# A gated recurrence in 128 steps: other queues for the first loads, biases loaded spread out, and plain units moved in the last steps

## The chip, the cores and the metric

The kernel runs on one core of a Trainium2 chip. The metric is the device time of one execution in microseconds, as the median of several runs; 0.2% of it is 2.7 us. The profile is that of one further execution with its own time. A core has five engines with queues of their own: TensorE (PE, with its weight loads as PEld), VectorE (DVE), ScalarE (ACT), GpSimd (POOL) and SyncE (SP). Loads and stores are issued here from SP's queue and from ScalarE's.

## The reference

A gated recurrent unit runs over 128 steps for 64 sequences with 512 inputs and 512 hidden values, and its outputs are added to the input:

```python
def step(h, inp):
    x_t, prop = inp
    comb = jnp.concatenate([x_t, h], axis=-1)
    z = jax.nn.sigmoid(comb @ Wz + bz)
    r = jax.nn.sigmoid(comb @ Wr + br)
    comb2 = jnp.concatenate([x_t, r * h], axis=-1)
    h_cand = jnp.tanh(comb2 @ Wh + bh)
    h_new = (1.0 - z) * h + z * h_cand
    h_next = jnp.where(prop, jnp.tanh(h_new @ Wp + bp), h_new)
    return (h_next, h_new)
```

`prop` holds at every fourth step except the last. The result is `x` plus all `h_new`. Everything is float32.

## The kernel before

**Layout.** The 64 sequences and two halves of the 512 hidden values together fill 128 partitions: partition `s * 64 + b` holds columns `256 s` to `256 s + 255` of sequence `b`. A product with one 128-row block of a weight matrix is two matmuls (`products`, L188), one for each half `s`, into the upper and the lower 64 partitions of PSUM; each is two float32 instructions of 256 columns. Such a pair of matmuls is called a unit. Four units make one gate of one step.

**The serial part.** A step multiplies h (turned into hT, k on partitions) by the lower rows of Wr, then Wz (`wh[0]`, `wh[1]`), takes sigmoids on ScalarE, forms `rh = r * h` on VectorE, turns it (`turn`, L213: eight transposes on TensorE and two copies), and multiplies it by the lower rows of Wh (`wh[2]`). Then come tanh, a multiplication by z and an addition of `keep = (1 - z) h`, each in two halves (c = 0, 1), and the turn of the new h, in two halves too. The slots for r and the candidate lie in one PSUM tile (`rc`), z's and the propagation's in another (`zp`). They are seeded ahead of the products with what x and the bias contribute to the step (`seed`, a ScalarE copy from `G[t]`), so that the products only accumulate.

**The parallel part.** What x contributes doesn't depend on h and fills TensorE's time while the other engines work through the chain. For steps 0 to 7 it is done plainly: `plain(t)` gives 12 units, four for each gate, from the upper rows of the weights (`wx`), and VectorE then adds the bias into `G[t]`. From step 8 to 123 four steps are taken together with sums of weights and sums of inputs that save products (`batch`, with GpSimd doing most additions). The last four steps are plain again (`plain_last`). The units stand in a list, and `fill(n)` issues the next n of them at the place where it is called. The program order written out by hand is thus the order of every engine; `manual_schedule` leaves it alone. `read_out()` emits the additions that take finished units out of PSUM.

**Places.** In steps up to 118 `PLACES` says how many units go to which place of a step. In the last nine steps, 119 to 127, `TAIL` does: its first triple holds the units ahead of the first half turn of h, between the two half turns, and behind the second. The second pair serves the propagation.

**The start.** Ten idle matmuls on zeros run while the first loads arrive. The four biases arrive as four rows in one partition (`bias_row`, which borrows the space of the weight sums `tt`). `spread` multiplies them by a row of ones, so that they stand in all 64 rows of each half in PSUM, directly in the slots of step 0, and copies them to `bias`. Then `turn_x` turns x of steps 0 and 1. Step 0's units accumulate straight into the biased slots, one by one alternating with the plain units of step 1. h's first state is turned after r's units. The upper rows of each weight matrix are loaded in two halves, the first on SP's queue and the second on ScalarE's. ScalarE's queue starts with the biases and carries the first state after its half of Wr. The lower rows all go on SP's queue, in the order r, x of steps 2 and 3, z, candidate.

**Order on the other engines around the change.** At step 3 VectorE does `sum_inner(5)` and `sum_inner_1(5)` (L320 to L325) after its copy for the turn of h and ahead of the read-out of a finished batch (L515 to L517). At step 127 ScalarE seeds the candidate's slot (L395, called at L666) ahead of the sigmoid of r (L675).

Of the kernel before, what the change touches and what calls it, by code (L numbers as in the profile page):

```python
# [9 lines left out]
F32 = mybir.dt.float32  # L10
BF16 = mybir.dt.bfloat16
# [6 lines left out]
def kernel(  # L18
# [29 lines left out]
    nc = tc.nc  # L48
# [20 lines left out]
    ps_c = ctx.enter_context(tc.tile_pool(name="ps_c", bufs=1, space=PSUM))  # L69
    ctx.enter_context(tc.manual_schedule())  # L70

    ident = const.tile([P, P], F32, name="ident")
    make_identity(nc, ident)
    ones = const.tile([1, B], F32, name="ones")
# [9 lines left out]
    tw = {n: const.tile([P, S, S, 3, P], F32, name=f"tw_{n}") for n in (2, 3, 4)}  # L84
    tt = const.tile([P, 7, 3, S, 3, P // 2], F32, name="tt")
    gates_in = (Wr, Wz, Wh)

    bias_row = tt.rearrange("p a b c d e -> p (a b c d e)")[0:1, : 4 * H].rearrange(
        "p (i n) -> p i n", i=4
    )  # L90

    def load_x(tile_, t0, n, j=0):
        for s in range(S):
            nc.sync.dma_start(
                out=tile_[s * B : (s + 1) * B, j : j + n, :], in_=x[:, t0 : t0 + n, ts(s, N)]
            )

    def load_w(wt, w, k0, k1, eng):
        eng.dma_start(
            out=wt[:, k0:k1, :],  # L100
            in_=w[k0 * P : k1 * P, :].rearrange("(k p) n -> p k n", p=P),
        )
# [3 lines left out]
    def new_xr(g):  # L106
        xr[g] = xrp.tile([P, Q4, N], F32, tag="xr", name=f"xr_{g}")

    for i, b in enumerate((br, bh, bz, bp)):
        nc.scalar.dma_start(out=bias_row[:, i, :], in_=b.rearrange("(o n) -> o n", o=1))  # L110
    h_init = two.tile([P, N], F32, tag="h", name="h_init")
    new_xr(0)
    load_x(xr[0], 0, 2)
    for i in range(3):
        for k in (0, 2):
            load_w(wx[:, :, i, :], gates_in[i], k, k + 2, nc.sync if k == 0 else nc.scalar)
        if i == 0:
            for s in range(S):
                nc.scalar.dma_start(out=h_init[s * B : (s + 1) * B, :], in_=h0[:, ts(s, N)])
    for i in range(3):  # L120
        for k in (0, 2):
            load_w(wh[i], gates_in[i][D:, :], k, k + 2, nc.sync)
        if i == 0:
            load_x(xr[0], 2, 2, 2)

    dummy = const.tile([1, 1], F32, name="dummy")
    nc.scalar.activation(dummy, ones[:, 0:1], AF.Sigmoid)
# [23 lines left out]
    act_ps = [ps[:, N : N + P] for ps in turn_ps]  # L151


    bias = const.tile([P, C, 4, P], F32, name="bias")

    def cut(ps):
        return ps.rearrange("p (c n) -> p c n", c=C)

    def spread(a, ps):
        for s in range(S):  # L160
            nc.tensor.matmul(  # L161
                ps[s * B : (s + 1) * B, :, :],
                lhsT=ones,
                rhs=bias_row[:, 2 * a : 2 * a + 2, ts(s, N)],
                start=True,
                stop=True,
            )
        for i in ((R, H_), (Z, 3))[a]:
            nc.vector.tensor_copy(bias[:, :, i, :], cut((slots[i] if i < 3 else slot_p)))  # L169

    bias0 = bias[:, 0, 0:3, :]
    bias_d = const.tile([P, 3, P], F32, name="bias_d")


    zeros = one.tile([P, 2 * N], BF16, tag="cq", name="zeros")
    nc.gpsimd.memset(zeros, 0.0)

    def idle(n):
        for _ in range(n):
            nc.tensor.matmul(  # L180
                scratch[0][:B, :], lhsT=zeros[:, :B], rhs=zeros, start=True, stop=True
            )


# [208 lines left out]
    def seed(i, t):  # L393
        if t < T:
            nc.scalar.copy(cut(slots[i]), G[t][:, :, i, :])  # L395
# [5 lines left out]
    def fill(n):  # L401
        for _ in range(min(n, len(queue))):
            unit, end = queue.pop(0)
            unit()
            if end is not None:
                pending.append(end)
# [5 lines left out]
    def plain(t):  # L412

        first, second = scratch[:2] if t % 2 == 0 else scratch[2:]
        regions = (first[:, :N], first[:, N:], second[:, :N])
        g, i = divmod(t, Q4)

        def end():
            new_cp(t // 2)
            nc.vector.tensor_add(  # L420
                G[t][:, :, 0:2, :],
                first.rearrange("p (g c n) -> p c g n", g=2, c=C),
                bias[:, :, 0:2, :],
            )
# [119 lines left out]
        nc.gpsimd.tensor_add(dst, a, b)  # L544

    def with_bias(g, i, v):
        m = M[g, i].rearrange("p b g u -> p b (g u)")
        nc.gpsimd.tensor_add(
            m, m, v.rearrange("p g u -> p (g u)").unsqueeze(1).to_broadcast([P, 2, 3 * P])
        )  # L550

    def c_block(g, a, nb):
# [28 lines left out]
    def outer_c21(g):  # L581
# [7 lines left out]


    TAIL = (
        ((4, 1, 0), (2, 1)), ((4, 1, 0), ()), ((4, 1, 0), ()), ((4, 1, 0), ()),
        ((4, 1, 0), (2, 1)), ((4, 1, 0), ()), ((5, 1, 2), ()), ((3, 1, 0), ()), ((0, 0, 0), ()),
    )


    idle(10)
    spread(0, rc)
    turn_x(0, nc.vector)
    turn_x(1, nc.vector)  # L600
    spread(1, zp)
    nc.gpsimd.tensor_sub(bias_d, bias[:, 1, 0:3, :], bias0)
    idle(2)
    h = h_init
    hT = new_T("hT", "hT_init")
    first = [
        [lambda e=e, k=k: product(slots[e], xT[0][:, 0], wx[:, :, e, :], k) for k in ORDER]
        for e in range(3)
    ]
    second = plain(1)  # L610
    for e in range(3):

        queue.extend(second[4 * e : 4 * e + 4])
        for n in range(4):
            first[e][n]()
            fill(1)
        if e == 0:
            for c in range(C):
                turn(h, hT, c, "hT_init", nc.vector)
    read_out()  # L620
# [3 lines left out]
    for t in range(T):  # L624
# [37 lines left out]
        if t < 6:  # L662
            turn_x((2, 5, 8, 11, 13, 15)[t])
        read_out()
        if t == T - 1:
            seed(H_, t)  # L666
        if u == 0 and pair >= 1 and odd - 2 < LAST:
            outer_u2(odd - 2)
        if t == 3:
# [4 lines left out]
        for c in range(C):  # L674
            nc.scalar.activation(act_ps[c], slots[R][:, ts(c, P)], AF.Sigmoid)  # L675
            nc.vector.tensor_mul(rh[:, ts(c, P)], act_ps[c], h[:, ts(c, P)])  # L676
        seed(R, t + 1)
        join(0)


# [12 lines left out]
        nc.scalar.activation(slots[Z], slots[Z], AF.Sigmoid, scale=-1.0)  # L693
        nc.vector.tensor_mul(keep, slots[Z], h)
        join(1)
        seed(Z, t + 1)
        if prop:
            nc.scalar.copy(cut(slot_p), bias[:, :, 3, :])
# [37 lines left out]
        fill(places[2] if thin else places[1] - 6)  # L736
        if t == 2:
            sum_outer_1()
        if t == 3:
            sum_inner(5, nc.vector)  # L740
            sum_inner_1(5, nc.vector)
        if prop:
            for k in ORDER:
                product(slot_p, hT, wp, k)
# [128 lines left out]
```

## Time and profile before

| what | us |
| --- | --- |
| median of three runs | 1343.7 |
| lowest and highest run | 1342.44, 1344.1 |
| the profiled execution | 1342.88 |
| its span, first to last instruction | 1341.0 |
| TensorE busy | 1329.3 |
| GpSimd busy | 908.7 |
| VectorE busy | 702.2 |
| ScalarE busy | 626.6 |

The span is what the profile's times count in; the execution's own time is 1.9 us longer. The mean granted TensorE clock is 0.998. A row of the timeline gives the start, the duration, the engine with the line, the operation, the tile written and the tiles read, the shape and how many instructions were merged; in brackets stands how long the engine sat idle ahead of it and what ended that. Lines are those of the kernel before. L188 is the matmul of `products`, L213 a transpose of `turn`, L204 the copy that follows it, L180 an idle matmul, L161 a bias matmul, L395 a seed. Matmuls overlap, so one row's duration is more than its share of TensorE's time: 16 instructions of 256 columns with 379 ns each take 1.73 us, hence 0.43 us for a unit.

### The profile page before, as it was taken

Reading aid. Unit: us, or ns where it says so; the run is one execution under the profiler, and the core shown is the slowest. Engines: PE = TensorE matmul, PEld = TensorE weight load, DVE = VectorE, ACT = ScalarE, POOL = GpSimd, SP = SyncE. Lnnn points to the kernel's source line nnn. Section 1 sums busy time; section 2 is a strip of 40 time slices with the busy share of each in tenths; the row PEclk is TensorE's granted clock in tenths of the full one; section 3 lists DMA queues with packets and bytes.
Section 4 is the critical chain, followed back from the end, with each engine's and each line's share of the span. In section 5 each row is a group of like instructions: output and inputs, shape, how many; then the busy total and the mean of one; then the engine's idle time right before and its main releaser. Section 6 shows DMA issues by size and latency. Waiting matters only on the chain.

```text
span 1341.0 us, 37605 instructions
## 1 busy us (share of the span) xinstructions
PE 1329.3 (99%) x15344; PEld 1113.4 (83%) x15344; DVE 702.2 (52%) x1868; ACT 626.6 (47%) x1848; POOL 908.7 (68%) x1111
## 2 busy tenths in 40 slices
PE   9999999999999999999999999999999999999998
PEld 6678888888888888888888888888888888888765
DVE  3355555555555555555555555555555555555444
ACT  1244545454554545455445454545445444554433
POOL 3448776777767777776787767787677687767400
PEclk9999999999999999999999999999999999999999
DMA  9011223122221222213212231222212222131300
GB/s 286 18 33 33 64 47 80 35 49 49 64 65 33 65 42 56 64 33 71 57 34 65 53 76 33 49 48 65 64 33 65 48 49 64 33 80 34 103 18 17
DMA packets 114868, 76.22 MB, mean 57 GB/s; under 512 B 61700, under 2 KB 109956, under 8 KB 114696
## 3 DMA queue, kind: packets, MB, share of 16 engines
q1 hardware_dynamic: 113632, 72.04, 23.2%
q8 instruction: 121, 1.98, 0.6%
q10 hardware_dynamic: 1064, 1.78, 0.4%
q14 instruction: 51, 0.42, 0.1%
HBM read 42.34 MB, written 16.78 MB: 44 GB/s over the span
## 4 chain that ended last, share of the span: by engine, by line
PE 99%; DVE 1%; issue 0%; ACT 0%; POOL 0%; DVEq 0%; POOLq 0%; ACTq 0%
PE rc L188 34%; PE zp L188 20%; PE scratch_q L188 11%; PE scratch_x L188 11%; PE scratch_r L188 10%; PE scratch_a L188 6%; PE turn L213 5%; PE scratch_q L180 0%; PE rc L161 0%; ACT xT L204 0%; PE zp L161 0%; DVE rh L676 0%; DVE turn L720 0%; DVE bias L169 0%; DVE h L725 0%
## 5 line engine op out<-in xcount | busy, mean ns | idle before, releaser
L188 PE MATMUL rc<-wh,rhT 128*64 128x256 f32 x2048 | 245.9, 379 | 0.0
L188 PE MATMUL zp<-wh,hT 128*64 128x256 f32 x1536 | 204.5, 379 | 0.0
L188 PEld LDWEIGHTS rc<-wh,rhT 128*64 128x64 f32 x2048 | 167.4, 137 | 41.1
L544 POOL TENSOR_TENSOR cp<-mb,mb 128x768 f32<-128x768 f32 x72 | 130.8, 1816 | 102.4 <-ACT rc L395 54.8
L188 PE MATMUL rc<-wh,hT 128*64 128x256 f32 x1536 | 186.4, 383 | 0.5
L805 POOL TENSOR_TENSOR xr<-xr,h 128x256 f32<-128x256 f32 x127 | 92.5, 728 | 113.5 <-DVE h L725 112.5
L188 PEld LDWEIGHTS rc<-wh,hT 128*64 128x64 f32 x1536 | 121.9, 137 | 36.5 <-issue 10.4
L544 POOL TENSOR_TENSOR cp<-mb 128x768 f32<-128x768 f32 x44 | 79.9, 1817 | 99.1 <-ACT rc L395 98.0
L720 DVE TENSOR_TENSOR turn<-turn,z 128x128 f32<-128x128 f32 x256 | 75.4, 295 | 129.1 <-ACT turn L719 127.6
L188 PEld LDWEIGHTS zp<-wh,hT 128*64 128x64 f32 x1536 | 119.1, 137 | 24.5
L204 DVE COPY rhT<-turn 128x256 uint16<-128x256 uint16 x256 | 97.6, 420 | 70.2 <-PE turn L213 69.1
L675 ACT ACTIVATE turn<-rc 128x128 f32<-128x128 f32 x256 | 55.4, 261 | 162.7 <-issue 110.1
L204 ACT COPY hT<-turn 128x256 uint16<-128x256 uint16 x127 | 47.3, 372 | 167.7 <-DVE hT L204 127.7
L544 POOL TENSOR_TENSOR mb<-mb,mb 128x768 f32<-128x768 f32 x58 | 105.5, 1820 | 10.7 <-DVE mb L517 10.7
L719 ACT ACTIVATE turn<-rc 128x128 f32<-128x128 f32 x256 | 55.5, 260 | 107.1 <-PE rc L188 107.0
L515 DVE TENSOR_TENSOR mb<-scratch_r,cq 128x384 f32<-128x384 f32 x102 | 56.7, 556 | 89.8 <-ACT cq L514 89.8
L508 DVE TENSOR_TENSOR cx<-scratch_r,cx 128x384 f32<-128x384 f32 x102 | 56.7, 556 | 88.2 <-ACT cx L506 88.2
L395 ACT COPY rc<-cp 128x256 f32<-128x256 f32 x254 | 95.6, 376 | 13.6 <-PE rc L188 1.7
L692 ACT ACTIVATE z<-zp 128x256 f32<-128x256 f32 x128 | 49.0, 383 | 95.1 <-PE zp L188 95.1
L274 ACT COPY xT<-xv 128x512 uint16<-128x512 uint16 x112 | 85.9, 767 | 0.0
L725 DVE TENSOR_TENSOR h<-turn,keep 128x128 f32<-128x128 f32 x254 | 74.1, 292 | 15.7 <-DVE turn L720 0.5
L213 PEld LDWEIGHTS <-h 128*64 128x64 bf16 x1016 | 68.2, 110 | 12.9 <-DVE h L725 4.6
(156 smaller groups left out, 3009.5 us busy)
## 6 DMA issues: line engine op xcount, KB each, us to landing
xr<-in_x_dram SPq DMA_DIRECT2D x62, 256.0 KB, 4.0
out_dram<-xr SPq DMA_DIRECT2D x62, 256.0 KB, 3.3
xs<-in_x_dram SPq DMA_DIRECT2D x56, 256.0 KB, 4.3
wh<-in_L_cond_Wr_dram SPq DMA_DIRECT2D x2, 512.0 KB, 7.7
wh<-in_L_cond_Wz_dram SPq DMA_DIRECT2D x2, 512.0 KB, 8.8
wh<-in_L_cond_Wh_dram SPq DMA_DIRECT2D x2, 512.0 KB, 11.4
early<-in_x_dram SPq DMA_DIRECT2D x4, 256.0 KB, 12.9
wp<-in_L_cond_Wp_dram SPq DMA_DIRECT2D x1, 1024.0 KB
```

Of the source, the lines that this page charges most:

```text
L188: nc.tensor.matmul(ps[s * B : (s + 1) * B], lhsT=lhs, rhs=rhs(s), start=start, stop=True, skip_group_check=True,)
L204: (eng.copy if eng is nc.scalar else eng.tensor_copy)(dst, src)
L213: nc.tensor.transpose(pt[s * B : (s + 1) * B, w, :], words.rearrange("p (n w) -> p w n", w=2)[:, w, :], ident16,)
L274: nc.scalar.copy(xT[g][:, i].bitcast(U16).rearrange("p c (n w) -> p w c n", w=2), xv[g][:, i])
L395: nc.scalar.copy(cut(slots[i]), G[t][:, :, i, :])
L508: nc.vector.tensor_add(T2[n][:, :nm], r_ps[:, :nm], T2[n][:, :nm])
L515: nc.vector.tensor_add(blocks()[:, :nm, 0, 1], r_ps[:, :nm], q2[:, :nm])
L544: nc.gpsimd.tensor_add(dst, a, b)
L719: nc.scalar.activation(pc, slots[H_][:, ts(c, P)], AF.Tanh)
L720: nc.vector.tensor_mul(pc, pc, z[:, ts(c, P)])
L725: nc.vector.tensor_add(h_new[:, ts(c, P)], pc, keep[:, ts(c, P)])
L805: nc.gpsimd.tensor_add(xr[g][:, j, :], xr[g][:, j, :], h_new)
```

## The change

- The loads: Wr's upper rows, both halves, go on ScalarE's queue, those of Wz and Wh on SP's. ScalarE's queue then carries the first state and the biases of r, z and the candidate; the bias of the propagation goes on SP's queue behind x of steps 2 and 3, ahead of Wz's lower rows.
- The biases: each is loaded twice, once for each half, with one row of 256 values repeated over 64 partitions, into `bias_in`. `spread`, its matmuls and its copies are gone. `bias` is a view of `bias_in` with the gate index outside the half, so the three gates of `bias0` are no longer contiguous, and `with_bias` on GpSimd uses a view with one more dimension.
- The start: the zeros are set by VectorE as its first instruction instead of by GpSimd. Idle matmuls number 16, 4 and 8 instead of 10 and 2, lie around the two turns of x, and write into the four half slots of `rc` and `zp` in turn. Step 0 becomes a plain step like step 1, with its units in scratch, its read-out and its three seeds; gate by gate the four units of step 0 come ahead of the four of step 1. The first state is turned after z's units.
- In the last nine steps the triple (4, 1, 0) becomes (3, 2, 0).
- Step 127 seeds the candidate's slot after the sigmoids of r.
- Step 3 does `sum_inner(5)` and `sum_inner_1(5)` right after `keep`.

```diff
+    zeros = one.tile([P, 2 * N], BF16, tag="cq", name="zeros")
+    nc.vector.memset(zeros, 0.0)
...
-    for i, b in enumerate((br, bh, bz, bp)):
-        nc.scalar.dma_start(out=bias_row[:, i, :], in_=b.rearrange("(o n) -> o n", o=1))
     h_init = two.tile([P, N], F32, tag="h", name="h_init")
+    bias_in = const.tile([P, 4, N], F32, name="bias")
     new_xr(0)
     load_x(xr[0], 0, 2)
     for i in range(3):
         for k in (0, 2):
-            load_w(wx[:, :, i, :], gates_in[i], k, k + 2, nc.sync if k == 0 else nc.scalar)
-        if i == 0:
-            for s in range(S):
-                nc.scalar.dma_start(out=h_init[s * B : (s + 1) * B, :], in_=h0[:, ts(s, N)])
+            load_w(wx[:, :, i, :], gates_in[i], k, k + 2, nc.scalar if i == R else nc.sync)
+
+    def load_bias(i, eng):
+        for s in range(S):
+            eng.dma_start(
+                out=bias_in[s * B : (s + 1) * B, i, :],
+                in_=(br, bz, bh, bp)[i][ts(s, N)]
+                .rearrange("(o n) -> o n", o=1)
+                .broadcast_to([B, N]),
+            )
+
+    for s in range(S):
+        nc.scalar.dma_start(out=h_init[s * B : (s + 1) * B, :], in_=h0[:, ts(s, N)])
+    for i in (R, Z, H_):
+        load_bias(i, nc.scalar)
     for i in range(3):
         for k in (0, 2):
             load_w(wh[i], gates_in[i][D:, :], k, k + 2, nc.sync)
         if i == 0:
             load_x(xr[0], 2, 2, 2)
+            load_bias(3, nc.sync)
...
-    bias = const.tile([P, C, 4, P], F32, name="bias")
+    bias = bias_in.rearrange("p i (c n) -> p c i n", c=C)
...
-    def spread(a, ps):
...
+    def idle(n):
+        for i in range(n):
+            s = i % S
             nc.tensor.matmul(
-                ps[s * B : (s + 1) * B, :, :],
-                lhsT=ones,
-                rhs=bias_row[:, 2 * a : 2 * a + 2, ts(s, N)],
+                (rc, zp)[i // S % 2][s * B : (s + 1) * B, :, :],
+                lhsT=zeros[:, :B],
+                rhs=zeros,
                 start=True,
                 stop=True,
...
     def with_bias(g, i, v):
-        m = M[g, i].rearrange("p b g u -> p b (g u)")
+        m = M[g, i]
         nc.gpsimd.tensor_add(
-            m, m, v.rearrange("p g u -> p (g u)").unsqueeze(1).to_broadcast([P, 2, 3 * P])
+            m, m, v.unsqueeze(1).to_broadcast([P, 2, 3, P])
         )
...
     TAIL = (
-        ((4, 1, 0), (2, 1)), ((4, 1, 0), ()), ((4, 1, 0), ()), ((4, 1, 0), ()),
-        ((4, 1, 0), (2, 1)), ((4, 1, 0), ()), ((5, 1, 2), ()), ((3, 1, 0), ()), ((0, 0, 0), ()),
+        ((3, 2, 0), (2, 1)), ((3, 2, 0), ()), ((3, 2, 0), ()), ((3, 2, 0), ()),
+        ((3, 2, 0), (2, 1)), ((3, 2, 0), ()), ((5, 1, 2), ()), ((3, 1, 0), ()), ((0, 0, 0), ()),
     )
...
-    idle(10)
-    spread(0, rc)
+    idle(16)
     turn_x(0, nc.vector)
+    idle(4)
     turn_x(1, nc.vector)
-    spread(1, zp)
+    idle(8)
     nc.gpsimd.tensor_sub(bias_d, bias[:, 1, 0:3, :], bias0)
-    idle(2)
     h = h_init
     hT = new_T("hT", "hT_init")
-    first = [
-        [lambda e=e, k=k: product(slots[e], xT[0][:, 0], wx[:, :, e, :], k) for k in ORDER]
-        for e in range(3)
-    ]
-    second = plain(1)
+    both = [plain(0), plain(1)]
     for e in range(3):
-
-        queue.extend(second[4 * e : 4 * e + 4])
-        for n in range(4):
-            first[e][n]()
-            fill(1)
-        if e == 0:
+        for us in both:
+            queue.extend(us[4 * e : 4 * e + 4])
+        fill(4)
+        if e == H_:
+            read_out()
+            seed(R, 0)
+            seed(Z, 0)
+            seed(H_, 0)
+        fill(4)
+        if e == Z:
             for c in range(C):
                 turn(h, hT, c, "hT_init", nc.vector)
     read_out()
...
-        if t == T - 1:
-            seed(H_, t)
...
         seed(R, t + 1)
+        if last:
+            seed(H_, t)
         join(0)
...
         join(1)
+        if t == 3:
+            sum_inner(5, nc.vector)
+            sum_inner_1(5, nc.vector)
         seed(Z, t + 1)
...
-        if t == 3:
-            sum_inner(5, nc.vector)
-            sum_inner_1(5, nc.vector)
```

More of the change, by code (lines that the diff above doesn't have):

```diff
@@ L86 @@
     gates_in = (Wr, Wz, Wh)
-    bias_row = tt.rearrange("p a b c d e -> p (a b c d e)")[0:1, : 4 * H].rearrange(
-        "p (i n) -> p i n", i=4
-    )
     def load_x(tile_, t0, n, j=0):
@@ L151 @@
     act_ps = [ps[:, N : N + P] for ps in turn_ps]
-    bias = const.tile([P, C, 4, P], F32, name="bias")
+    bias = bias_in.rearrange("p i (c n) -> p c i n", c=C)
     def cut(ps):
         return ps.rearrange("p (c n) -> p c n", c=C)
-    def spread(a, ps):
-        for s in range(S):
+    bias0 = bias[:, 0, 0:3, :]
+    bias_d = const.tile([P, 3, P], F32, name="bias_d")
+    def idle(n):
+        for i in range(n):
+            s = i % S
             nc.tensor.matmul(
-                ps[s * B : (s + 1) * B, :, :],
-                lhsT=ones,
-                rhs=bias_row[:, 2 * a : 2 * a + 2, ts(s, N)],
+                (rc, zp)[i // S % 2][s * B : (s + 1) * B, :, :],
+                lhsT=zeros[:, :B],
+                rhs=zeros,
                 start=True,
                 stop=True,
[L167 to L181, printed above, removed]
             )
```

## The prediction

> **What bounds the kernel now.** I read the page's busy times and the chain that ended last, then TensorE's own waits, because only they can move the end; then the stages and the DMA of the start, and the timeline around each remaining wait.
>
> ```profile
> PE 1329.3 (99%) x15344; PEld 1113.4 (83%) x15344; DVE 702.2 (52%) x1868; ACT 626.6 (47%) x1848; POOL 908.7 (68%) x1111
> ...
> PE 99%; DVE 1%; issue 0%; ACT 0%; POOL 0%; DVEq 0%; POOLq 0%; ACTq 0%
> ```
>
> ```profile
> PE turn L213 <- DVE rh L676: 2.7, 3, 1.4
> PE scratch_q L180 <- POOL zeros L176: 1.9, 1, 1.9
> PE turn L213 <- DVE xT L204: 0.8, 1, 0.8
> PE scratch_r L188 <- DVE mb L515: 0.4, 1, 0.4
> PE turn L213 <- DVE h L725: 0.2, 1, 0.2
> ```
>
> The waits give us in total, times, and the longest. TensorE is the chain for 99% of the span and waits 6 us in all. The change keeps every product of the recurrence, so it can only win in the first 25 us, at single stalls, and in the last steps. Nothing between 107 and 1250 us waits on TensorE, and nothing there is changed in size.
>
> The start, first by stage (after the engines' busy times: granted clock, DMA share, GB/s), then by DMA rate in 40 slices of 0.75 us over the first 30 us:
>
> ```profile
> 10.00:11.00 1.00, 1.00 (x8) 0.41 (x5) 0.40 (x2) 0.00 (x0) 0.00 (x0) 0.69 1.04 347
> ...
> 12.00:13.00 1.00, 1.00 (x7) 0.53 (x4) 0.00 (x0) 0.00 (x0) 0.10 (x1) 0.50 1.06 391
> ...
> 14.00:15.00 1.00, 1.00 (x14) 0.78 (x10) 0.00 (x0) 0.00 (x0) 0.00 (x0) 1.00 1.05 385
> ```
>
> ```profile
> GB/s 0 0 3 180 142 119 283 325 363 396 408 382 335 337 365 385 391 385 393 382 388 341 249 246 243 377 385 396 377 380 371 232 240 210 229 205 231 250 272 336
> ...
> wh<-in_L_cond_Wz_dram SPq DMA_DIRECT2D x2, 512.0 KB, 8.8
> ```
>
> The first product starts at 10.47 and runs at half clock until 13.8 (0.50). The DMA engines move 380 to 395 GB/s of weights without a break from 6 us on, and only 205 to 250 GB/s where the rows are 1 KB (x, at 17 and at 24 us). So the start has two bounds, TensorE's preparation and the stream of weights. In the issue records the second half of Wz's lower rows goes out at 14.06 and lands 8.8 later, at 22.8; its product starts at 25.46 (z's first unit at 25.03, plus 0.43). That is 2.6 us of slack for the weights.
>
> **The start, worked out.** Removed: eight bias matmuls (1.39 + 1.08 us of TensorE) and four DVE copies of 0.42. Added: 16 more idle matmuls, and two DVE additions (0.69 and 0.42) and three ScalarE copies (0.38 each) that seed step 0.
> TensorE: the zeros now come from VectorE's first instruction. No row shows that memset on VectorE; I bound it by GpSimd's ident (0.20) below and the 0.59 of VectorE's cast above, and take the upper end as the same engine's, so the idles begin near 1.2 instead of 1.90. Idle matmuls now alternate the two 64-column halves as products do. Products overlap in twos (16 of 379 ns in 1.73 us), so I count 8 times 0.43 for the 16: until 4.6 (all one after another, 8.1). x's two halves land 3.6 us after their issue, about 5.3; then eight transposes (0.4), four idles (0.9), the second step's transposes once VectorE has copied the first (7.0), eight idles (1.7 at half clock). The first product starts at **8.8**. r's second half, whose two halves landed at 7.9 and 8.4, then hides behind the idles. From there 24 units of 0.43 (10.4), the turn of the first state (0.3), step 0's r products (1.73) and a turn of x (0.23) put z's first unit at 21.5 and its second at 21.9. The seeds hide: the first addition needs only r's and z's units of step 0, which end twelve units before step 0 begins; behind the first state's turn and copies some six are left (2.6 us, against 0.69 + 0.38). Without that cover they would cost 1.1.
> The stream: eight bias loads of 64 rows of 1 KB are 0.52 MB where 8 KB were. At the 230 GB/s of x's rows that is 2.3 us ahead of Wz's lower rows. In return both queues hold large transfers from their first issue; the slices from 2.25 to 6.75 us fall short of 385 by 0.67 MB (1.75 us), and I give back 1.0 of it. Wz's second half lands at 22.8 + 2.3 - 1.0 = **24.1**, later than TensorE's 21.9. A stall of 2.2 us takes the place of the removed preparation: that product starts at 24.2 instead of 25.46, a gain of **1.3**. If all landed in time the gain would be 25.46 - 21.9 = 3.6; if the ramp gives nothing back, 0.3. Wz's upper rows, Wh and r's lower rows have one to two microseconds of room on the same count. Wh's lower rows (before: landed 27.1, wanted 32.7) stay hidden. On ScalarE's queue the six bias loads stand ahead of the table load (1.28); the first two loads of h_init took 2.24 to issue, so the queue is done near 12 to 14, before the seeds at 17.
> Here the Trainium skill speaks against the change ("DMA: Bandwidth & Descriptors", Issuing engines are not separate DMA queues): loads issued from different engines share the same DMA engines and save only issue time. The row agrees: 388 GB/s at 12 to 15 us with two queues, 377 to 396 at 19 to 22 with SP's alone. By the rule all 0.52 MB counts (1339.7 below). Were ScalarE's queue a path of its own, SP's would carry two more halves of upper rows, one less, and bp: 0.66 MB at 385, 1.7 us, and the sum would be 1339.1. I take the rule.
> The clock: the same skill ("TensorE: Matmul & The Clock Gate", Part 1) has half rate return after an idle window of some 3.4 us. The row at 10 us shows it after a stretch with much less idling (TensorE busy 1.13 of 2 us from 8 to 10, mostly transposes and one-row bias matmuls). By the rule the 2.2 us stall costs nothing; by that row it could cost 3.4 us at half clock, 1.7 us, giving 1341.4. Nearer is the stall at 102.5 to 105, busy 1.07 of 2.5, at clock 1.00. I take nothing. A cold clock at 8.8 itself would cost 1.7, and is covered by the same stall.
>
> **Step 3's sums** (`sum_inner(5)` and its in-place step), in the timeline:
>
> ```profile
> 84.14 0.55 DVE L320 TENSOR_TENSOR tt<-wx 128x384 f32<-128x384 f32 x1
> ...
> 86.26 0.55 DVE L515 TENSOR_TENSOR mb<-scratch_r,cq 128x384 f32<-128x384 f32 x1
> ...
> 86.96 0.55 PE L188 MATMUL scratch_r<-tw,s 128*64 128x192 f32 x4 [0.39 <-DVE mb L515]
> ```
>
> Four DVE operations (84.14 to 86.34) stand before the read-out at L515, and TensorE, done with wp's products at 86.41, starts at 86.96: 0.55 late, and 0.1 more of drain. Moved behind `keep` (which ends at 78.85) they run to 81.05. VectorE's next is L508 at 80.20, then L509, then the candidate's multiplication at 82.36; L508 and L509 shift by 0.85 to end at 82.1, just before it, and their banks are wanted again only at 83.15 and 84.02. Gain **0.6**; if the cover failed, the multiplication would be a few tenths late.
>
> **The last steps**, step 120 as the example of the form (4, 1):
>
> ```profile
> 1275.39 0.29 DVE L725 TENSOR_TENSOR h<-turn,keep 128x128 f32<-128x128 f32 x1
> ...
> 1276.15 0.28 PE L213 MATMUL turn<-ident,h 128*64 128x128 bf16 x4
> ...
> 1276.69 0.28 PE L213 MATMUL turn<-ident,h 128*64 128x128 bf16 x4
> ...
> 1277.05 0.44 PE L188 MATMUL rc<-wh,hT 128*64 128x256 f32 x2
> ```
>
> The second turn takes 0.11 and ends at 1276.80; the next products wait for VectorE's copy of the first until 1277.05, 0.25. With three units ahead the first turn comes at 1275.74 (half h is done at 1275.69; three units end at 1275.72), its copy 0.9 later at 1276.64, and two units with the second turn end at 1276.85. The 0.25 goes, 0.02 to 0.08 comes back where h's half is the later. Six steps have the form (4, 1): 6 x 0.20 = **1.2**. The second half's copy keeps 0.1 of room.
>
> And the last step, 127:
>
> ```profile
> 1332.07 0.38 ACT L395 COPY rc<-cp 128x256 f32<-128x256 f32 x1 [1.71 <-PE rc L188]
> ...
> 1332.47 0.43 ACT L675 ACTIVATE turn<-rc 128x128 f32<-128x128 f32 x2
> ...
> 1333.11 0.31 PE L213 MATMUL turn<-ident,rh 128*64 128x128 bf16 x4 [0.27 <-DVE rh L676]
> ```
>
> In the last step the seed (0.38, with its gap 0.41) stands before the sigmoid, and TensorE waits from 1332.65 to 1333.11. Behind the sigmoids it is done at 1332.9, before the candidate's products at 1333.8. Gain **0.4**.
>
> **Edits at nothing.** bias0 now has a step between gates. GpSimd's 58 bias additions take 1.82 with either operand; its additions over stepped views (L352, 0.73) take as long as over plain ones (L805, 0.73), and TensorE never waits for it after the start. VectorE's additions with bias (0.68) and ScalarE's copy for slot_p keep their sizes.
>
> **Sum.** 1.3 + 0.6 + 1.2 + 0.4 = 3.5. The profiled execution took 1342.9 (span 1341.0), which gives 1339.4; the median shown, 1343.7, gives 1340.2. I take 1339.7 between them. A change under 0.2% (2.7 us: faster means under 1341.0) can't be told from none here.
>
> **Rivals.**
> The forecast, stall at Wz's lower rows: 1338.6 to 1341.0, chance 0.50.
> Weights in time: the start gains 3.6 and the whole 5.8, 1337.4. For it: the ramp loss is 1.75, and repeated rows of one bias may be read faster than x's. Against: the slowest part of a transfer sets its landing, and 0.52 MB is sure. 0.22.
> The start gives nothing: a long stall with the clock dropping (1.7), or idle matmuls that don't overlap (first product at 11 to 14). The other places still give 2.2: 1341.0 to 1342.8. For it: the half clock at 10 us. 0.20.
> Slower: loads that read one row 64 times. No row shows one. It decides when the eight cost 8.6 us instead of 2.3 (0.52 MB at 61 GB/s): Wz's half then lands at 30.4 and 5 us of stall outweigh the 2.2 elsewhere, for 1346.0 and up. Against: the write side is 1 KB rows, as x's. 0.08.
> That fills 8 in 10 between 1337.0 and 1342.0; the likeliest case alone spans 1338.6 to 1341.0. Faster 0.72, same 0.20, slower 0.08.
>
> **What would show it.** First product near 8.8; TensorE waiting 1.5 to 2.5 us ahead of z's second unit in step 0, for a DMA; r's next start under 0.15 after a second turn in the last steps; L515 right after L514 in step 3; the sigmoid at once after r's products in step 127. The prediction is wrong if step 0's z products don't wait, if the clock falls after a stall, or if a new wait appears at steps 4 to 120.

## The result, and the profile after

The changed kernel takes 1340.76 us (median of 18 runs, 1339.82 to 1341.68), the kernel before 1343.59 in the same series (18 runs, 1342.44 to 1345.62). The ratio is 0.998, with a 95% interval from 0.9974 to 0.9986: 2.8 us faster, 0.21%. Forecast were 1339.7 and a gain of 3.5. The profiled execution of the changed kernel took 1341.68 (span 1339.9) and is the slowest of its 18, which matters below.

TensorE is as full as before, and the chain that ended last is still its own. First the busy times, then the chain by engine:

```profile
PE 1326.0 (99%) x15352; PEld 1109.8 (83%) x15352; DVE 702.1 (52%) x1867; ACT 627.3 (47%) x1851; POOL 910.8 (68%) x1110
...
PE 98%; DMA 1%; DVE 0%; issue 0%; ACT 0%; SPq 0%; DVEq 0%; ACTq 0%
```

The new entry is 1% DMA. TensorE's waits (us in all, times, longest) say where it is:

```profile
PE turn L211 <- DMA xr<-in_x_dram: 4.5, 1, 4.5
PE turn L211 <- DVE rh L671: 2.4, 2, 1.4
PE rc L174 <- DVE zeros L73: 1.2, 1, 1.2
PE turn L211 <- DVE h L725: 0.2, 1, 0.2
```

The wait for `mb` in step 3 (0.4) is gone, one of the three waits for `rh` too, and the zeros are there 0.7 earlier. Against that stands one wait of 4.5 for x. On TensorE's timeline of the start:

```profile
4.18 0.44 PE L174 MATMUL zp<-zeros 128*64 128x512 bf16 x2
9.10 0.64 PE L211 MATMUL turn<-ident,xr 128*64 128x128 bf16 x8 [4.48 <-DMA xr<-in_x_dram]
...
12.48 1.95 PE L186 MATMUL scratch_q<-wx,xT 128*64 128x256 f32 x8
```

The idle matmuls end at 4.62, as counted (4.6). But x's second half lands at 8.96 by the landing records of the trace, not at 5.3, so the first product starts at 12.48 instead of the forecast 8.8, and later than before, where it starts at 10.47:

```profile
10.47 0.69 PE L188 MATMUL rc<-wx,xT 128*64 128x256 f32 x1
```

By stage (granted clock, DMA share and GB/s are the last three columns), and then the DMA rate in slices of 0.75 us over the first 30 us:

```profile
10.00:11.00 1.00, 1.00 (x14) 0.81 (x12) 0.48 (x2) 0.00 (x0) 0.00 (x0) 0.50 1.01 350
...
12.00:13.00 1.00, 1.00 (x8) 0.62 (x6) 0.00 (x0) 0.36 (x1) 0.00 (x0) 0.50 1.06 267
...
14.00:15.00 1.00, 1.00 (x9) 0.61 (x7) 0.00 (x0) 0.14 (x1) 0.00 (x0) 0.73 0.98 178
```

```profile
GB/s 0 0 131 188 239 281 262 265 313 270 176 269 309 309 346 238 277 317 213 174 277 369 399 382 391 378 243 245 228 346 382 399 396 391 388 306 210 228 208 214
```

The clock is half from 7.70 to 14.53 here, twice as long as in the profile of before (10.38 to 13.79). From 6 to 15 us the queues move 174 to 346 GB/s where before they moved 335 to 408. In this execution z's second unit of step 0 starts at 26.47, 0.43 after the first, behind TensorE's own work and not behind a load: 1.0 later than before (25.46). Here are z's first three units, before and then after:

```profile
25.03 0.38 PE L188 MATMUL zp<-wh,hT_init 128*64 128x256 f32 x1
...
25.08 1.46 PE L188 MATMUL zp<-wh,hT_init 128*64 128x256 f32 x11
```

```profile
26.04 1.48 PE L186 MATMUL zp<-wh,hT_init 128*64 128x256 f32 x12
```

The three late places look as forecast. Step 3 (`L515` of before is L513 here), on three engines:

```profile
85.48 0.48 ACT L512 COPY cq<-scratch_q 128x384 f32<-128x384 f32 x1
...
85.64 1.90 PE L186 MATMUL zp<-wp,hT 128*64 128x256 f32 x16
86.00 0.56 DVE L513 TENSOR_TENSOR mb<-scratch_r,cq 128x384 f32<-128x384 f32 x1 [0.82 <-ACT cq L512]
...
87.37 0.49 PE L186 MATMUL scratch_r<-tw,s 128*64 128x192 f32 x4
```

VectorE now waits for ScalarE's copy, adds at once, and TensorE's next product has no wait in brackets. But the four sums take 3.0 us at their new place (79.72 to 82.74) where the old one took 2.2. GpSimd adds at the same time there, and both engines are slower. One operation of each, before (VectorE's while GpSimd stood idle) and then after:

```profile
79.68 0.73 POOL L360 TENSOR_TENSOR o<-xT 128x256 f32<-128x256 f32 x1
...
85.79 0.55 DVE L325 TENSOR_TENSOR wx<-wx 128x384 f32<-128x384 f32 x1
```

```profile
81.28 1.04 POOL L358 TENSOR_TENSOR o<-xT 128x256 f32<-128x256 f32 x1
...
81.66 1.08 DVE L323 TENSOR_TENSOR wx<-wx 128x384 f32<-128x384 f32 x1
```

Step 120 on TensorE, around the second half turn of h, and step 127 on ScalarE:

```profile
1276.47 0.60 PE L186 MATMUL scratch_q<-wx,xT 128*64 128x256 f32 x4
1276.90 0.28 PE L211 MATMUL turn<-ident,h 128*64 128x128 bf16 x4
1277.02 0.82 PE L186 MATMUL rc<-wh,hT 128*64 128x256 f32 x6
```

```profile
1331.10 0.43 ACT L670 ACTIVATE turn<-rc 128x128 f32<-128x128 f32 x2 [1.66 <-PE rc L186]
...
1331.56 0.38 ACT L393 COPY rc<-cp 128x256 f32<-128x256 f32 x1
```

r's products follow the start of the turn after 0.12 instead of 0.36, and the sigmoid goes before the seed.

From one execution alone I read: the late places gain 2.2, the start loses 1.0. The first half of that held; the second did not.

### The profile page after: what moved, and what is told of

It is laid out like the page before. It is cut to its first block, busy times and chain, and to the rows that moved or that the text cites. A ratio compares the mean times of both kernels' runs of the same rounds, so it can differ in the third digit from the quotient of the medians.

```text
span 1339.9 us, 37622 instructions
## 1 busy us (share of the span) xinstructions
PE 1326.0 (99%) x15352; PEld 1109.8 (83%) x15352; DVE 702.1 (52%) x1867; ACT 627.3 (47%) x1851; POOL 910.8 (68%) x1110
## 4 chain that ended last, share of the span: by engine, by line
PE 98%; DMA 1%; DVE 0%; issue 0%; ACT 0%; SPq 0%; DVEq 0%; ACTq 0%
PE rc L186 33%; PE zp L186 20%; PE scratch_q L186 11%; PE scratch_r L186 11%; PE scratch_x L186 11%; PE scratch_a L186 6%; PE turn L211 5%; DMA xr<-in_x_dram 1%; ACT xT L202 0%; PE zp L174 0%; PE rc L174 0%; DVE turn L720 0%; SPq L91 0%; DVE h L725 0%; DVE xr L723 0%
## 5 line engine op out<-in xcount | busy, mean ns | idle before, releaser
L542 POOL TENSOR_TENSOR mb<-mb,mb 128x768 f32<-128x768 f32 x58 | 105.5, 1819 | 10.5 <-DVE mb L515 10.5
L513 DVE TENSOR_TENSOR mb<-scratch_r,cq 128x384 f32<-128x384 f32 x102 | 56.7, 556 | 90.5 <-ACT cq L512 90.5
```

The costliest lines, as they stand in the source:

```text
L513: nc.vector.tensor_add(blocks()[:, :nm, 0, 1], r_ps[:, :nm], q2[:, :nm])
```

## The experiments

All times stand beside runs of the kernel before on the same chip; ratios are to it. Every kernel does the whole computation. Where the bias loads are issued twice, the added tile is read by nothing. A landing is the time at which the last of a load's sixteen semaphore events arrives.

**The late edits alone** (on the kernel before):

```diff
-        ((4, 1, 0), (2, 1)), ((4, 1, 0), ()), ((4, 1, 0), ()), ((4, 1, 0), ()),
-        ((4, 1, 0), (2, 1)), ((4, 1, 0), ()), ((5, 1, 2), ()), ((3, 1, 0), ()), ((0, 0, 0), ()),
+        ((3, 2, 0), (2, 1)), ((3, 2, 0), ()), ((3, 2, 0), ()), ((3, 2, 0), ()),
+        ((3, 2, 0), (2, 1)), ((3, 2, 0), ()), ((5, 1, 2), ()), ((3, 1, 0), ()), ((0, 0, 0), ()),
...
-        if t == T - 1:
-            seed(H_, t)
...
         seed(R, t + 1)
+        if last:
+            seed(H_, t)
...
         join(1)
+        if t == 3:
+            sum_inner(5, nc.vector)
+            sum_inner_1(5, nc.vector)
...
-        if t == 3:
-            sum_inner(5, nc.vector)
-            sum_inner_1(5, nc.vector)
```

> The kernel before with the three late edits alone (step 3's sums, the form (3, 2, 0) in six steps, the last seed behind the sigmoids). By the prediction's own terms these give 0.6 + 1.2 + 0.4 = 2.2 us, so 1341.4 if the kernel before has 1343.6. If they give the whole 2.8 us of the change, the new start is worth nothing; if less than 1.5, one of the three terms is wrong. In the trace: the start as before (first product near 10.5), the stall at L515 gone, less than 0.15 us from a second half turn to r's products in the last steps.

1341.60 (18 runs), ratio 0.9984 (0.9977 to 0.9991): 2.1 us faster. Read from the traces, each stretch being from a step's first r product to another's, the last one to the start of TensorE's last instruction:

| stretch | before | after | late edits alone | forecast gain | gain |
| --- | --- | --- | --- | --- | --- |
| step 3 to step 4 | 15.88 | 15.33 | 15.33 | 0.6 | 0.55 |
| step 119 to step 125 | 55.78 | 54.57 | 54.56 | 1.2 | 1.22 |
| step 127 to the last instruction | 5.71 | 5.26 | 5.26 | 0.4 | 0.45 |

The three terms are 2.2 in the trace. They add up, and they are the same in the changed kernel.

**The start alone** (the changed kernel with those edits undone):

```diff
-        ((3, 2, 0), (2, 1)), ((3, 2, 0), ()), ((3, 2, 0), ()), ((3, 2, 0), ()),
-        ((3, 2, 0), (2, 1)), ((3, 2, 0), ()), ((5, 1, 2), ()), ((3, 1, 0), ()), ((0, 0, 0), ()),
+        ((4, 1, 0), (2, 1)), ((4, 1, 0), ()), ((4, 1, 0), ()), ((4, 1, 0), ()),
+        ((4, 1, 0), (2, 1)), ((4, 1, 0), ()), ((5, 1, 2), ()), ((3, 1, 0), ()), ((0, 0, 0), ()),
...
+        if t == T - 1:
+            seed(H_, t)
...
-        if last:
-            seed(H_, t)
...
-        if t == 3:
-            sum_inner(5, nc.vector)
-            sum_inner_1(5, nc.vector)
...
+        if t == 3:
+            sum_inner(5, nc.vector)
+            sum_inner_1(5, nc.vector)
```

> The changed kernel with the three late edits undone: the new start alone. Theory (x is late): the trace of the changed kernel has z's second unit of step 0 at 26.47 instead of 25.46, a loss of 1.0, so about 1344 to 1344.6. The prediction's step (a stall at Wz's lower rows, a gain of 1.3) would give 1342.3. Start and late edits are far apart in time, so the two parts should add up to the whole change.

1342.09 (15 runs), ratio 0.9986 (0.9978 to 0.9994): 1.6 us faster. So the start gains, and my reading of a loss, taken from the changed kernel's one profile, falls. TensorE's timeline at z's first two units of step 0:

```profile
23.74 0.62 PE L186 MATMUL zp<-wh,hT_init 128*64 128x256 f32 x4
24.60 1.08 PE L186 MATMUL zp<-wh,hT_init 128*64 128x256 f32 x8 [0.25 <-DMA wh<-in_L_cond_Wz_dram]
```

Here the forecast wait exists: the second half of Wz's lower rows lands at 24.56 and its product starts at 24.60. The clock was half for one window only (7.68 to 11.10), and x's second half landed at 7.78. The gains of the two halves, 2.1 and 1.6, make 3.7 where the whole has 2.8; each interval is about 1 us to either side, so the parts don't contradict the whole.

**x ahead of Wr.** x's second half goes first on ScalarE's queue:

```diff
-    load_x(xr[0], 0, 2)
+    for s, eng in enumerate((nc.sync, nc.scalar)):
+        eng.dma_start(out=xr[0][s * B : (s + 1) * B, 0:2, :], in_=x[:, 0:2, ts(s, N)])
```

> The changed kernel with the two halves of x for steps 0 and 1 first on both queues, the second half on ScalarE's ahead of Wr. Theory (x is late because Wr's transfers on the other queue go ahead of it): x lands before 5.5, TensorE's wait of 4.5 us goes, the first product starts near 9, and Wz's lower rows become the bound (25.6 in the changed kernel): a gain of 0.8 on the changed kernel, about 1340.0, up to 2 more if the stream moves forward too. Rival (the 0.52 MB of repeated bias rows slow the stream and x's place doesn't matter): the same time as the changed kernel, 1340.8.

1340.75 (11 runs), ratio 0.9977 (0.9968 to 0.9986): the time of the changed kernel. x lands at 3.63 and 4.32, the first product starts at 6.58, and then:

```profile
6.58 0.63 PE L187 MATMUL scratch_q<-wx,xT 128*64 128x256 f32 x4
10.29 2.17 PE L187 MATMUL scratch_q<-wx,xT 128*64 128x256 f32 x12 [3.08 <-DMA wx<-in_L_cond_Wr_dram]
```

Wr's second half comes at 10.25 instead of 8.15. The gain of 0.8 that the expectation named did not come; its rival had the time right. The wait went from x to Wr. z's second unit starts at 24.96 against a landing at 24.92: a first product 4.6 to 5.9 us earlier than with the change's own order (11.20 in the start alone, 12.48 in the changed kernel) gains nothing in the median.

**Wr in quarters.** Four transfers of 256 KB instead of two of 512 KB:

```diff
-        for k in (0, 2):
-            load_w(wx[:, :, i, :], gates_in[i], k, k + 2, nc.scalar if i == R else nc.sync)
+        n = 1 if i == R else 2
+        for k in range(0, K, n):
+            load_w(wx[:, :, i, :], gates_in[i], k, k + n, nc.scalar if i == R else nc.sync)
```

> The changed kernel with Wr's upper rows in four transfers of 256 KB instead of two of 512 KB, same queue, same bytes. If the DMA engines take the two queues' transfers in turn, whole transfer by whole transfer, x's second half waits behind two quarters instead of two halves and lands near 6.5 instead of 8.96, and the first product starts some 2 us earlier. If the queues share packet by packet, or the sheer bytes decide, x lands at 8.5 to 9 as before and the time stays at 1340.8.

1341.46 (15 runs), ratio 0.9981 (0.9973 to 0.9988): no better than the changed kernel. x's second half lands at 6.83 instead of 7.66 to 8.96 with the changed kernel's loads. So what held x back are Wr's transfers on the other queue, and their size counts: two queues take turns by large pieces. The packet records of the start alone show such turns: SP's queue moves the 128 packets of x's first half from 3.5 us on, 122 of them by 4.5, and none from 5.0 to 5.5; from 4.5 to 5.5 ScalarE's moves 126 of Wr; then x's second half follows. The Trainium skill ("DMA: Bandwidth & Descriptors", Queues, rings and completion order) says that a DMA engine drains a whole packet from one queue before it turns to the next; the trace agrees in kind, and no run here shows the size of a packet. The first product starts at 10.35, and z's two units at 23.41 and 24.72, right behind landings at 23.37 and 24.68. The end of the start is again the stream's.

**The bias loads twice** (0.52 MB more):

```diff
+    spare = const.tile([P, 4, N], F32, name="spare")
...
-        for s in range(S):
+        for to, s in [(to, s) for to in (bias_in, spare) for s in range(S)]:
             eng.dma_start(
-                out=bias_in[s * B : (s + 1) * B, i, :],
+                out=to[s * B : (s + 1) * B, i, :],
```

> The changed kernel with every repeated bias load issued twice, the second into a tile that nothing reads: 0.52 MB more in the stream and nothing else. If the landing of Wz's lower rows bounds the start (theory), its landing and z's second unit of step 0 move from about 24.6 to about 26.9 and the time rises by 2.3, to 1343. If TensorE's own preparation (x late, half clock) bounds it, the time stays within 0.6 of 1340.8.

1344.84 (13 runs), ratio 1.0008 (0.9999 to 1.0016): 4.1 us more than the changed kernel (3.8 by the ratios). The direction is that of the theory; the size, 2.3, was missed.

```profile
27.76 0.65 PE L187 MATMUL zp<-wh,hT_init 128*64 128x256 f32 x4 [2.55 <-DMA wh<-in_L_cond_Wz_dram]
29.05 1.08 PE L187 MATMUL zp<-wh,hT_init 128*64 128x256 f32 x8 [0.64 <-DMA wh<-in_L_cond_Wz_dram]
```

The issue records give a reason. The loads use eight semaphores in turn, on both queues together, and each load is issued only when the one eight before it has landed: the first bias load goes out at 5.41, the first half of Wr landed at 5.38. With sixteen bias loads among them SP issues Wz's lower rows at 23.38, against 16.29 to 17.80 in the three executions with the changed kernel's loads, and its first half lands at 27.72 instead of 22.93 to 24.24, 4.3 later than their mean. Just ahead of that issue the DMA engines have little to do (the last two columns are their busy share and GB/s):

```profile
22.00:23.00 1.00, 1.00 (x12) 0.75 (x10) 0.60 (x1) 0.38 (x1) 0.92 (x2) 1.00 0.35 82
23.00:24.00 1.00, 1.00 (x14) 0.69 (x12) 0.42 (x1) 0.00 (x0) 0.92 (x2) 1.00 0.37 126
```

In the changed kernel the share is 1.02 and 1.06 in the same two stretches. So a small load can cost a place among eight as well as its bytes; this run does not part the two costs.

**Less ahead of Wz.** x of step 3 and the propagation's bias go behind the lower rows of Wz and Wh (0.26 MB less ahead):

```diff
         if i == 0:
-            load_x(xr[0], 2, 2, 2)
+            load_x(xr[0], 2, 1, 2)
+        if i == 1:
+            load_x(xr[0], 3, 1, 3)
+        if i == 2:
             load_bias(3, nc.sync)
```

> The changed kernel with x of step 3 and the propagation's bias loaded behind Wz's and Wh's lower rows: 0.26 MB less ahead of Wz's. Theory (the stream bounds): Wz's second half lands 1.1 us earlier and the time falls by 0.5 to 1.1, to about 1340.0; TensorE's preparation as the bound: 1340.8.

1339.85 (7 runs), ratio 0.9973 (0.9963 to 0.9984), 0.9 below the changed kernel, with overlapping intervals. The landing moved to 23.57, and z's second unit starts at 24.34, with no wait:

```profile
23.90 1.48 PE L189 MATMUL zp<-wh,hT_init 128*64 128x256 f32 x12
```

TensorE, at half clock from 7.76 to 11.18, came later than the stream. So the two bounds of the start lie about one us apart, and moving one finds the other.

**More idle matmuls** (36 instead of 16 ahead of x):

```diff
-    idle(16)
+    idle(36)
```

> The changed kernel with 36 idle matmuls ahead of the first turn of x instead of 16, so that TensorE doesn't rest while x is on its way. If the half clock at the start is covered by the stall at Wz's lower rows, as the prediction has it, the median stays at 1340.5 to 1340.8 and only the slowest runs (1341.2 and above) come down. If the clock is what costs, the time falls by 1 or more.

1340.86 (11 runs), ratio 0.9976 (0.9967 to 0.9985): the time of the changed kernel. After 4.18 the clock is full throughout, the first product starts at 9.92, and all of it runs into the stall:

```profile
22.98 0.65 PE L186 MATMUL zp<-wh,hT_init 128*64 128x256 f32 x4 [0.32 <-DMA wh<-in_L_cond_Wz_dram]
24.33 1.08 PE L186 MATMUL zp<-wh,hT_init 128*64 128x256 f32 x8 [0.70 <-DMA wh<-in_L_cond_Wz_dram]
```

The landings are at 22.93 and 24.29. A full clock earlier in the start is worth nothing at the median: there the stream sets the end of the start, not TensorE. The expectation had the median right; the slowest runs, which were to come down, go up to 1343.02.

**Bias rows kept, x first on both queues.** The kernel before with the late edits, and four bias rows of 2 KB behind x's halves, two on each queue. The zeros come from VectorE, and idle matmuls in pairs (16, 4 and 2) lie around the two turns of x. Step 0's units still go straight into the biased slots:

```diff
+    zeros = one.tile([P, 2 * N], BF16, tag="cq", name="zeros")
+    nc.vector.memset(zeros, 0.0)
...
-    for i, b in enumerate((br, bh, bz, bp)):
-        nc.scalar.dma_start(out=bias_row[:, i, :], in_=b.rearrange("(o n) -> o n", o=1))
...
-    load_x(xr[0], 0, 2)
+    both = (nc.sync, nc.scalar)
+    for s in range(S):
+        both[s].dma_start(out=xr[0][s * B : (s + 1) * B, 0:2, :], in_=x[:, 0:2, ts(s, N)])
+    for i, b in enumerate((br, bh, bz, bp)):
+        both[i % 2].dma_start(out=bias_row[:, i, :], in_=b.rearrange("(o n) -> o n", o=1))
...
-        for _ in range(n):
+        for i in range(n):
+            s = i % S
             nc.tensor.matmul(
-                scratch[0][:B, :], lhsT=zeros[:, :B], rhs=zeros, start=True, stop=True
+                scratch[i // S % 2][s * B : (s + 1) * B, :],
...
-    idle(10)
-    spread(0, rc)
+    idle(16)
     turn_x(0, nc.vector)
+    idle(4)
     turn_x(1, nc.vector)
+    spread(0, rc)
     spread(1, zp)
```

> The kernel before with the three late edits, the biases still as four rows and spread by matmuls, but x first on both queues, zeros from VectorE and idle matmuls in pairs (16, 4 and 2). Theory: without the 0.52 MB Wz's lower rows land at 21.5 to 22.8, x near 4.5, and the first product starts between 8.4 (full clock) and 9.5 (half clock), so z's second unit starts between 21.5 and 24 and the time is 1338 to 1340.5. Rival (the 1-row bias matmuls leave the clock at half and cost more than the stream gives): 1341 to 1342, as with the late edits alone.

1337.54 (5 runs, 1336.84 to 1338.65), ratio 0.9954 (0.994 to 0.9967): 6.1 below the kernel before and 3.2 below the changed one. It is the fastest version here.

```profile
4.61 0.64 PE L220 MATMUL turn<-ident,xr 128*64 128x128 bf16 x8
...
8.45 0.60 PE L195 MATMUL rc<-wx,xT 128*64 128x256 f32 x4
```

```profile
21.28 0.65 PE L195 MATMUL zp<-wh,hT_init 128*64 128x256 f32 x4
22.63 1.08 PE L195 MATMUL zp<-wh,hT_init 128*64 128x256 f32 x8 [0.70 <-DMA wh<-in_L_cond_Wz_dram]
```

x is there when the idles end, the first product starts at 8.45, and Wz's lower rows land at 22.59, 1.7 to 3.0 earlier than with the repeated bias loads. The end of the start is still a landing. The bias matmuls and the preparation that the change removed cost nothing in this execution, since TensorE waits 0.70 for Wz all the same. "x ahead of Wr" has x first too; against it the landing is 2.3 earlier and the time 3.2 lower. The two differ in the biases' path, but also in step 0's units and in the queues of the upper rows.

**The same, with x of step 3 behind Wz's lower rows:**

```diff
-        if i == 0:
-            load_x(xr[0], 2, 2, 2)
+        if i < 2:
+            load_x(xr[0], 2 + i, 1, 2 + i)
```

> The version with four bias rows and x first on both queues, and x of step 3 loaded behind Wz's lower rows: 0.13 MB less ahead of them. That version still waited 0.65 us for Wz's second half (landed 22.59, second unit at 22.63). Theory (the stream bounds it): the landing moves 0.5 forward and the time falls by 0.3 to 0.6, to about 1337.0. If TensorE bounds it: 1337.5.

1338.91 (5 runs), ratio 0.9963 (0.9951 to 0.9976): no better, a miss. In its profile the landing is at 22.52, z's second unit starts at 22.89 without a wait, and the clock was half from 7.80 to 11.21:

```profile
22.45 1.48 PE L195 MATMUL zp<-wh,hT_init 128*64 128x256 f32 x12
```

TensorE was the bound in this execution, so nothing was to be had. With five runs of each, the difference of 1.2 (by the ratios) from the version above is not settled.

**The same preparation, loads on the queues of before:**

```diff
-    both = (nc.sync, nc.scalar)
-    for s in range(S):
-        both[s].dma_start(out=xr[0][s * B : (s + 1) * B, 0:2, :], in_=x[:, 0:2, ts(s, N)])
     for i, b in enumerate((br, bh, bz, bp)):
-        both[i % 2].dma_start(out=bias_row[:, i, :], in_=b.rearrange("(o n) -> o n", o=1))
+        nc.scalar.dma_start(out=bias_row[:, i, :], in_=b.rearrange("(o n) -> o n", o=1))
+    load_x(xr[0], 0, 2)
```

> The kernel before with the three late edits and only the preparation on TensorE changed: zeros from VectorE, idle matmuls in pairs (16, 4 and 2) around the turns of x, both bias spreads behind the second turn. All loads on the queues of before. If the preparation is what the version with x first gained by (first product at 8.45 at full clock instead of 10.5 at half), this one has 1337.5 to 1338.2 as well; if x first on both queues gave it, 1340 to 1341.6.

1340.04 (5 runs, 1337.57 to 1342.5), ratio 0.9966 (0.9952 to 0.9979). The runs of this kernel lie 5 us apart, and the profiled one is the slowest:

```profile
5.84 0.64 PE L218 MATMUL turn<-ident,xr 128*64 128x128 bf16 x8 [1.03 <-DMA xr<-in_x_dram]
...
7.69 1.97 PE L163 MATMUL rc<-tt,ones 1*64 1x512 f32 x4
9.45 1.92 PE L163 MATMUL zp<-tt,ones 1*64 1x512 f32 x4
...
11.72 1.06 PE L193 MATMUL rc<-wx,xT 128*64 128x256 f32 x4
```

The time is the one expected if x's order gives the gain (1340 to 1341.6). x comes 1.0 too late, the eight bias matmuls take 3.9 instead of 2.1, and the four instructions of a unit take 1.06 instead of 0.60 until 17.0: TensorE runs at half rate all that time. How much of the 1.6 (by the ratios) between this and the fastest version is x's order on the queues, and how much the clock that follows from it, stays open.

## Why the prediction was right, and where its sum was off

**The late places (2.2 forecast).** Right term by term: 0.55, 1.22 and 0.45 against 0.6, 1.2 and 0.4. The cover named for the turn's second half held. The one for the moved sums did not quite: they took 3.0 us instead of 2.2 beside GpSimd's additions, and the candidate's multiplication came 3.79 behind the end of `keep` where it was 3.51, the few tenths that the prediction named for this case. TensorE had room for it: its turn of h comes 4.62 behind the end of `keep` in both kernels. No new wait appeared between steps 4 and 119: that stretch is 1167.93 before and 1167.86 after.

**The stall at Wz's lower rows.** The mechanism was right: where TensorE was ready, z's second unit began 0.04 behind the landing (24.60, 24.33, 24.72, 24.96 in four kernels; forecast 24.2), doubling the bias loads moved it to 29.05, and leaving them out to 22.63. The stall also hid TensorE's preparation, as forecast, since neither an earlier x nor a full clock changed the time. But in the changed kernel's own profile two of the prediction's signs of being wrong stand: z's products don't wait, and the clock falls after a stall, the one for x that the prediction did not have. The stall at z is seen in the other executions, not in that one.

**The size of the start (1.3 forecast).** Two terms were off. "I give back 1.0 of it" is the one that weighs. In the three executions with exactly the changed kernel's loads (changed kernel, start alone, more idles) Wz's second half lands at 25.60, 24.56 and 24.29, 24.8 in the mean. In the three with the loads of before (kernel before, late edits alone, old queues) it lands at 22.82, 21.50 and 22.90, 22.4 in the mean. So 2.4 are paid for the 0.52 MB, about the 2.3 counted, and nothing comes back, as far as three executions each, 1.3 to 1.4 apart, can tell. The slices show where the 1.0 went: the ramp did bring something, but it is lost again. In the changed kernel 1.16 MB move from 2.25 to 6.75 us instead of 1.06 (1.32 and 1.37 in the other two), and 2.4 MB from 6.75 to 15.75 (2.9 in the other two) instead of 3.4. The prediction read that stretch of before as 380 to 395 GB/s without a break; its own row has 335 and 337 at 9.0 to 10.5.

Why 64 rows of 1 KB move more slowly is not shown. They are short, but they also fill only 64 of the 128 partitions, and no run parts the two. A packet of 1 KB takes 46 ns at the median from 22 to 24 us in the run with the bias loads twice, and 80 ns from 24 to 26 us in the kernel before, where x is loaded; one of 2 KB takes 84 to 93 ns from 4 to 16 us of before. So a short packet is not slow by itself.

The second term is "x's two halves land 3.6 us after their issue": in the changed kernel they took 5.5 and 7.4, since Wr's transfers, issued at the same time on the other queue, went between them. So the first product started at 9.92 to 12.48 in the three executions, not at 8.8. It is mostly hidden, and that is luck in part: the sum had counted on 2.2 of cover for something else, the clock. Where the half clock lasts two windows, as in the changed kernel's profile, the cover fails: z's second unit starts at 26.47 although its rows landed at 25.60, and 0.9 is lost.

**The whole.** The 2.8 measured less the 2.2 of the late places leaves 0.6 for the start; the start alone measured 1.6 (0.8 to 3.0). Both lie between the forecast's ends for it (0.3 and 3.6), and 1.3 lies inside the second's interval and at the edge of the first's (1.9 to 3.5 for the whole). In the traces z's second unit starts at 26.47, 24.60 and 24.33 with the change's start, and at 25.46 and 26.25 with the start of before (late edits alone), 0.7 earlier in the mean. The likeliest case was the right one. "Weights in time" fell: the repeated rows were in all no cheaper than x's. "The start gives nothing" was the profiled execution, by late x and a long half clock. "Slower" fell: 0.52 MB of repeated rows cost 2.4, and not the 8.6 from which it would have decided.

**The two queues.** The rule that a second queue is no path of its own held: Wz's rows landed no earlier for it (24.8 in the mean; 24.1 was the forecast by the rule), and Wr on ScalarE's queue held back x on SP's.

## What to carry to other kernels

In a start that loads weights, find the landing that is waited for last and count the bytes and the loads ahead of it; what engines do meanwhile is worth nothing as long as it ends before that landing. Put what is wanted first at the head of every queue, since a large transfer on the other queue takes its turn in between. That alone only moved the wait here, from x to Wr; the fastest version also has fewer bytes ahead of the last landing. Before a loss of one us in one profile of a start is explained, run the halves of the change apart: here one trace showed a loss where the runs had a gain.

## What the runs showed of the hardware that was not expected

- In the start the half clock comes in windows of 3.41 us or a multiple (3.41 and 6.83 in the clock records). It began at 7.68 to 7.80 in four executions, and at 8.55, 10.38 and 11.01 in three. The Trainium skill ("TensorE: Matmul & The Clock Gate", Part 1: The HAM clock gate) has a free-running window of this length; the length agrees, and the four beginnings so close together leave open whether it runs freely here. The runs of one kernel lie 2 to 5 us apart.
- Being busy is not enough for the clock. In the last experiment TensorE shows no idle time from 6.2 to 17, 3.9 of it one-row bias matmuls, and stays at half rate until 17.0, for three windows' length. The page has the full rate return after one busy window; the trace fits that only if some of this work does not count, and no run here tests which. The 3.41 us just ahead of 17.01 are the first that hold products alone. The granted clock column reads 1.00 there, since the trace has no clock record before 17.01: durations (1.06 for 0.60) are the better witness at the start of a trace.
- A wait of 3.08 (7.21 to 10.29, Wr, x ahead of Wr) was followed by a half-clock window from 11.01; of the 3.41 us just before it 2.7 were idle. Waits of 2.55 and 0.64 (bias loads twice) were followed by none.
- Loads wait for the load eight before them, over both queues together: twice as many bias loads cost 4.1 us, not 2.3, and left the DMA engines at a share of 0.35 and 0.37 from 22 to 24 us.
- VectorE and GpSimd can slow each other: beside one another, VectorE's four sums took 3.0 us instead of 2.2, and four of GpSimd's additions 0.77 to 1.05 instead of 0.46 and 0.73 each. At the old place, in the kernel before and in the start alone, a sum took 0.55. VectorE's read-outs from PSUM (L508, L509 of before, 0.56) overlapped GpSimd's additions there and slowed neither.
- The landing of one and the same load lay between 24.29 and 25.60 in three executions, and between 21.50 and 22.90 in the three with the loads of before. Its sixteen semaphore events come 1.1 to 2.5 us apart from first to last, so the slowest of them sets the landing.
